# One gathered row in sixteen chunks moves from GpSimd's indirect DMA to 128 single fetches issued by SyncE

## The chip, the cores and the metric

The kernel runs on one core of a Trainium2 chip. The metric is the device time of one execution in microseconds (us). The kernel before takes 6118.95 us (median of 10 runs, 6115.97 to 6129.21); the profiled execution took 6118.65 us, of which the profile's span, from the first to the last instruction, is 6116.9 us.

Engines are named as in the profile: PE (TensorE, matmul), PEld (its weight load), DVE (VectorE), ACT (ScalarE), POOL (GpSimd), SP (SyncE, which here does nothing but issue DMAs and wait).

## What is computed

Two layers of a "metaformer" on x of 4 images x 128 channels x 128 x 128 positions, float32. Cut to what matters:

```python
# layer 0
x = x + deform_conv(ln_c(x), w_off, w_conv)      # 3x3 deformable convolution
t = tokens(x); t = t + moe_top2(ln_t(t), router_w, router_b, expert_w, expert_b)
# layer 1
x = x + conv(ln_c(x), alphas)                     # a 1x1 mixing with a reversal of rows and columns
t = tokens(x); t = t + moe_by_expert(ln_t(t), gate_w, gate_b, weight1, weight2)

def bilinear_gather(x, py, px):                   # in deform_conv, for each of 9 taps
    y0, x0 = floor(py), floor(px)                 # py, px: position + tap + learned offset
    return sum of 4 corners of x at (y0|y0+1, x0|x0+1), each times its bilinear weight
```

Each output position needs, for each of 9 taps, four neighbouring input positions (128 channels each) at an address that is known only at run time.

## The kernel before, in words

**The table.** For each image a table in DRAM holds, at each of 129 x 130 positions, the 256 floats (1 KB) of two normalised pixels above each other. Two neighbouring entries, 2 KB, are the four corners of one sample. `positions` (L651) computes the index of every sample into `im.index`, a [128, 128, 9] int32 tile (x on the partitions, then row y and tap k).

**The gathers.** Each image is worked in 32 groups of four rows (`row_groups`, L162), each group in 9 chunks, one for each tap: 4 x 32 x 9 = 1152 chunks. `Chunk.gather` (L771) issues four indirect DMAs on POOL, one for each row of the chunk; each brings 128 x 2 KB (256 KB) into a quarter of a tile `g`. There are 4608 of them. `g` has AHEAD = 6 buffers (L248), and the gathers are recorded six chunks ahead of their use.

**A chunk's way.** `weighted` (L784) multiplies three of its rows by the corner weights on DVE; `weighted_too` (L792) multiplies the fourth, `g[:, 3]`, on ACT (for k > 0; for k = 0 DVE takes all four). `summed` (L800) transposes and adds the four corners on PE (16 matmuls `trg`), `moved` (L814) copies the result to `sT` on ACT, `convolved` (L734) multiplies by the tap's weights into `sums` on PE. After 9 taps `mixed` (L823) does the rest of the layers for the four rows.

**The order.** All work is recorded in one loop over chunks (two half-steps, "turns", a chunk), and `InOrder` (L94) keeps each engine's instructions in just this order. Jobs (`turns.start`) are generators that yield for a number of turns. Tiles and semaphores are placed by a framework; a DMA issued from SP or ACT takes one of eight completion semaphores in rotation, and is not issued before the DMA eight places earlier, which used the same semaphore, has landed.

**SP's queue.** SP issues, in order, for every group the load of its four input rows (`xg`, 256 KB) and the store of its result (`x_d`, 256 KB); while the next image's table is built (`block`, L530), one load `xc` (512 KB) and one store `table<-ent` (1 MB) for each 8 rows; in the last image also expert weights (`w<-in_weight`, `pad<-in_weight`), and the last pass over finished images (`w<-x_d`, `out<-w`, 512 KB each). It waits, in that order, for whatever each of these needs.

**Padding tiles.** `padding` (L458) copies transposed rows into one of four tiles `pads` (L332), which `offsets` (L467) reads three times shifted for the offset convolution. Later the four are room for expert weights (`flat_pads`, L335, in `rooms` L1655 and `others` L1680).

Of the kernel before, what the change touches and what calls it, by code (L numbers as in the profile page):

```python
# [42 lines left out]
F32 = mybir.dt.float32  # L43
I32 = mybir.dt.int32
U32 = mybir.dt.uint32
AF = mybir.ActivationFunctionType
ALU = mybir.AluOpType
AX = mybir.AxisListType
# [3 lines left out]
P = 128  # L52
# [5 lines left out]
HID = 512  # L58
# [6 lines left out]
TAPS = 9  # L65
EPS_C = 1e-6
EPS_T = 1e-5
RB = 8
CB = 16
TW = P + 1  # L70
TC = P + 2
# [14 lines left out]
BANKS = 6  # L86
AFTER = 11
SPACE = 13
BLOCK = 84
FILL = "fill"  # L90
DONE = "done"
# [98 lines left out]
def metaformer_kernel(  # L190
# [50 lines left out]
    with ExitStack() as main:  # L241
# [100 lines left out]
        blank = wts.tile([P, P], F32, name="blank")  # L342
        nc.vector.memset(blank, 0.0)
        flip = wts.tile([P, P], F32, name="flip")
        nc.gpsimd.memset(flip, 0.0)
        for base in (0, -P):
# [108 lines left out]
                yield from with_bias(ew_sb[:, 4 * h : 4 * h + 4, :], biases[h])  # L455


        def padding(t, h, row, read, padded):  # L458

            yield FILL  # L460
            tr = transposes(row, 4)
            read.append(h)
            yield turns.hop
            eng.scalar.copy(pads[(2 * t + h) % 4][:, :, 1 : P + 1], tr)
            padded.append(h)

        def offsets(im, t, padded):  # L467

            while len(padded) < 2:
                yield 1  # L470
            yield 1


            yield FILL
            po = bank([P, 4, P], "po")
            for k in range(3):
                for h in range(2):
                    eng.tensor.matmul(
                        po[h * P // 2 : (h + 1) * P // 2],
                        lhsT=woff_sb[:, k, :],  # L480
                        rhs=pads[(2 * t + h) % 4][:, :, k : k + P],
                        start=(k == 0),
                        stop=(k == 2),
                    )
            yield turns.hop
# [13 lines left out]
            yield turns.hop  # L499
            if i0 == 0:  # L500
                im.z[q] = pa.tile([P, CB + 2, 6 * TAPS], F32, name=f"z{im.b}_{q}", tag="z")
                if q == 0:
                    eng.vector.memset(im.z[q][:, 0, :], 0.0)
                else:
                    eng.scalar.copy(im.z[q - 1][:, CB + 1, :], tr[:, 0, 0, 0 : 6 * TAPS])
            eng.scalar.copy(
                im.z[q][:, 1 + i0 : 1 + i0 + RB, :].rearrange("p (h i) o -> p h i o", h=2),
                tr[:, :, :, 0 : 6 * TAPS].rearrange("p i h o -> p h i o"),
            )
            if i0 == 0 and q > 0:  # L510
# [192 lines left out]
        class Group:  # L703
# [30 lines left out]
            def convolved(self, k):  # L734

                yield 1
                if k + 1 < FIRST:
                    return
                if k + 1 == FIRST:
                    eng.tensor.matmul(  # L740
                        sums.rearrange("p s c -> p (s c)"),
                        lhsT=blank,
                        rhs=iota,
                        start=True,
                        stop=False,
                    )
# [13 lines left out]
                if k + 1 == TAPS:  # L760
                    yield turns.hop
                    yield from mixed(self)

        class Chunk:


            def __init__(self, group, k):
                self.group, self.k = group, k
                self.shared = k > 0

            def gather(self):  # L771
# [12 lines left out]
            def weighted(self):  # L784
                n = 3 if self.shared else 4
# [4 lines left out]
                )  # L790

            def weighted_too(self):  # L792
                g, y = self.g[:, 3], self.group.rows[3]
                w = self.group.im.weight[y // CB]
                for v in range(4):
                    eng.scalar.activation(
                        g[:, v, :], g[:, v, :], AF.Copy, scale=w[:, y % CB, self.k, v : v + 1]
                    )

            def summed(self):  # L800

                self.tr = bank([P, 4, P], "trg")
                for s in range(4):
                    for v in range(4):
                        eng.tensor.matmul(
                            self.tr[:, s, :],
                            lhsT=self.g[:, s, v, :],
                            rhs=ident,
                            is_transpose=True,
                            start=(v == 0),  # L810
                            stop=(v == 3),
                        )

            def moved(self):  # L814
# [2 lines left out]
                eng.scalar.copy(group.sT[self.k], self.tr)  # L817
                turns.start(group.convolved(self.k))


        exps = []

# [766 lines left out]

        def in_turn():  # L1590

            for b in range(NB):
                for number, (rows_of, minus, runs) in enumerate(orders[b]):
                    im = images[b]
                    if im.sent <= P // RB or not im.weight.keys() >= {y // CB for y in rows_of}:
                        raise ValueError("a table is late")
                    group = Group(images[b], number, rows_of, minus, runs)
                    group.begin()
                    for k in range(TAPS):
                        chunk = Chunk(group, k)  # L1600
                        chunk.gather()
                        yield chunk

        source = in_turn()
        chunk = [next(source) for _ in range(AHEAD)]
        turns.hop = HOP
# [5 lines left out]
        def tick(more):  # L1612

            turns.fills(0)
            turns.slot += 1
            if more and total - QUICK <= n <= total:
                turns.steps()
                turns.fills(0)
                turns.slot += 1

        while n < total + 3 or turns.jobs:
# [134 lines left out]
```

## Time and profile before

| | us |
|---|---|
| median of 10 runs | 6118.95 |
| profiled execution | 6118.65 |
| its span | 6116.9 |
| PE busy | 5444.3 (89%) |
| DVE busy | 4846.0 (79%) |
| POOL busy | 4467.9 (73%) |
| ACT busy | 3821.4 (62%) |
| software DMA queue (POOL's gathers), share of 16 DMA engines | 64.4% |
| hardware DMA queue (SP's transfers, and ACT's few), share of 16 DMA engines | 14.2% |

A POOL instruction `DMA_INDIRECT g<-table,index` is the making of one gather's descriptors; the transfer itself runs on the 16 DMA engines afterwards. For SP, the profile lists only the issue of a DMA (named SPq); "to landing" is the time from the start of the issue until the last of the data is there.

### The profile page before, as it was taken

What the parts mean: (1) busy time and instruction counts of PE and PEld (TensorE: products, weight loads), DVE (VectorE), ACT (ScalarE), POOL (GpSimd) and SP (SyncE); (2) the same over time, 40 slices, a digit from 0 to 9 for tenths busy, and PEclk for the clock granted to TensorE, in tenths of its full rate; (3) what the DMA queues carried; (4) which work ended last, traced back from release to release, by engine and by line L of the source; (5) the groups of instructions that cost most, each with busy time, mean ns of one, the idle gap of its engine ahead of it and who ended that gap; (6) DMA issues with size and microseconds to landing.
All of it is one profiled execution on the core that took longest, in us unless ns stands there. A gap on an engine that the chain in (4) does not pass through costs nothing.

```text
span 6116.9 us, 118020 instructions
## 1 busy us (share of the span) xinstructions
PE 5444.3 (89%) x38823; PEld 4444.7 (73%) x38823; DVE 4846.0 (79%) x15420; ACT 3821.4 (62%) x9910; POOL 4467.9 (73%) x4795
## 2 busy tenths in 40 slices
PE   6899999998899999988889999999888998999984
PEld 4777777777777777777777777777777687777763
DVE  5688888887788888887778888888788787888872
ACT  4566666665666666666666666666655565666652
POOL 5777777777777777777777777777777777777750
PEclk8999999999999999999999999999999999999987
DMA  7778787877777777777777778777777897999777
GB/s 234 228 238 256 240 254 243 254 236 224 240 242 242 247 240 246 251 235 224 230 246 247 240 245 248 238 244 250 221 227 214 292 339 217 323 340 321 224 227 273
DMA packets 579234, 1526.15 MB, mean 249 GB/s; under 512 B 86456, under 2 KB 225408, under 8 KB 578624
## 3 DMA queue, kind: packets, MB, share of 16 engines
q0 software_dynamic: 369664, 1210.35, 64.4%
q1 hardware_dynamic: 206656, 299.87, 14.2%
q8 instruction: 310, 5.08, 0.3%
q10 hardware_dynamic: 2304, 8.39, 0.3%
q14 instruction: 300, 2.46, 0.1%
HBM read 1381.43 MB, written 136.85 MB: 248 GB/s over the span
## 4 chain that ended last, share of the span: by engine, by line
PE 30%; DMA 26%; DVE 16%; ACT 10%; issue 9%; POOL 9%; DVEq 0%; ACTq 0%; POOLq 0%; SPq 0%
DMA g<-table,index 23%; PE trg L104 10%; PE sums L104 9%; POOL g L104 8%; PE pe L104 6%; DVE g L104 5%; DVE x L104 5%; ACT g L104 4%; PE po L104 2%; PE tr L104 2%; DMA out<-w 2%; ACT sT L104 1%; ACT L104 1%; ACT xn L104 1%; PE small L104 1%
## 5 line engine op out<-in xcount | busy, mean ns | idle before, releaser
L104 POOL DMA_INDIRECT g<-table,index x4608 | 4368.7, 948 | 1409.5 <-issue 985.1
L104 DVE TENSOR_TENSOR g<-g,small 128x1536 f32<-128x1536 f32 (+1 forms) x1152 | 2083.1, 1809 | 901.4 <-DMA g<-table,index 773.3
L104 PE MATMUL trg<-ident,g 128*128 128x128 f32 x18432 | 2266.5, 277 | 155.2 <-DVE g L104 63.4
L104 PEld LDWEIGHTS trg<-ident,g 128*128 128x128 f32 x18432 | 2102.5, 144 | 275.1 <-DVE g L104 68.7
L104 ACT ACTIVATE g<-g,weight 128x128 f32<-128x128 f32 x4096 | 1306.2, 391 | 842.8 <-DMA g<-table,index 832.6
L104 DVE SCALAR_TENSOR_TENSOR x<-pe,gate,x 128x128 f32<-128x128 f32 x4072 | 1388.9, 343 | 83.3 <-PE pe L104 29.9
L104 PEld LDWEIGHTS sums<-wconv_sb,sT 128*128 128x128 f32 x9216 | 1139.6, 194 | 333.1 <-ACT sT L104 179.2
L104 PE MATMUL sums<-wconv_sb,sT 128*128 128x128 f32 x9216 | 1215.5, 280 | 131.8 <-ACT sT L104 130.3
L104 PE MATMUL pe<-ew_sb,nT 128*128 128x512 f32 x2048 | 1052.3, 612 | 177.4 <-ACT sT L104 151.2
L104 ACT COPY sT<-trg 128x512 f32<-128x512 f32 x1152 | 653.2, 568 | 98.6 <-PE trg L104 97.6
L104 PEld LDWEIGHTS pe<-ew_sb,nT 128*128 128x128 f32 x2048 | 330.8, 194 | 349.7 <-ACT sT L104 202.4
L104 ACT ACT_TABLE_LOAD x263 | 337.4, 1283 | 7.5 <-DVE nmax L104 2.2
L104 ACT ACTIVATE xn<-x,c_nb,c_rs 128x128 f32<-128x128 f32 x512 | 211.3, 485 | 167.3 <-DVE c_nb L104 167.2
L104 ACT ACTIVATE n<-x,b_nb,b_rs 128x128 f32<-128x128 f32 x512 | 210.3, 482 | 129.8 <-DVE b_nb L104 62.9
L104 ACT ACTIVATE c_rs<-c_mv,eps_c 128x4 f32<-128x4 f32 x128 | 37.9, 296 | 401.6 <-DVE c_mv L104 398.3
L104 ACT ACTIVATE tn<-x,d_nb,d_rs 128x128 f32<-128x128 f32 x512 | 210.9, 483 | 75.2 <-DVE d_nb L104 75.1
L104 PE MATMUL po<-pad,woff_sb 128*64 128x512 f32 x768 | 193.0, 621 | 21.8 <-DVE x L104 19.2
L104 PEld LDWEIGHTS sums<-ident,xg 128*128 128x128 f32 x1024 | 151.7, 212 | 77.7 <-issue 77.1
L104 ACT ACTIVATE ent<-raw,a_nb,a_rs 128x128 f32<-128x128 f32 x384 | 158.0, 484 | 16.1 <-DVE a_nb L104 14.3
L104 PEld LDWEIGHTS ps<-aT_sb,xfT 128*128 128x128 f32 x1024 | 130.1, 197 | 47.5 <-ACT xfT L104 37.1
L104 PE MATMUL ps<-aT_sb,xfT 128*128 128x128 f32 x1024 | 142.7, 284 | 22.0 <-ACT xfT L104 19.2
L104 PE MATMUL sums<-iota,blank 128*128 128x512 f32 x256 | 157.6, 702 | 0.0
(236 smaller groups left out, 5126.6 us busy)
## 6 DMA issues: line engine op xcount, KB each, us to landing
g<-table,index POOLq DMA_INDIRECT x4608, 3.8
table<-ent SPq DMA_DIRECT2D x48, 1024.0 KB, 6.4
xc<-in_x SPq DMA_DIRECT2D x64, 512.0 KB, 6.5
w<-x_d SPq DMA_DIRECT2D x64, 512.0 KB, 6.6
xg<-in_x SPq DMA_DIRECT2D x124, 256.0 KB, 7.3
x_d<-x SPq DMA_DIRECT2D x124, 256.0 KB, 4.2
out<-w SPq DMA_DIRECT2D x48, 512.0 KB, 8.0
w<-in_weight SPq DMA_DIRECT2D x42, 512.0 KB, 10.2
```

What stands on the lines that cost most here:

```text
L104: return self.tc.keep_in_program_order(issue(*args, **kwargs))
```

## The change

About one row in 64 is no longer gathered by POOL. For one chunk in sixteen, the fourth row is fetched by SP, in 128 DMAs of 2 KB, one for each x. This is done 71 times. A class `Lone` plans it while the program is recorded: it picks the user chunk n, a tap k > 0, so that the row is ready some eight chunks before; DVE multiplies the 128 indices by 1024 (bytes of a table entry); SP stores them in DRAM (`found`) and loads them again as a [4, 32] tile (`places`); then, for every 16 of them, one instruction loads 16 SP registers, and 16 DMAs follow, each from a register's byte offset in the table to one partition of a row tile. Five such DMAs are recorded each turn, so a row's 128 DMAs spread over 26 turns (13 chunks) of the 32 turns of a period. They stand in SP's queue among the other transfers.

Two of the four padding tiles (`pads[2:]`, "apart") become the two row tiles. In the main loop `padding` then has two tiles, and waits while they are in use (`busy`); as room for expert weights the two are replaced by two buffers of the pool `pw`. The tile `blank` goes, `zeros` takes its place.

```diff
+        apart = [
+            pad.rearrange("p y x -> p (y x)")[:, 0:HID].rearrange("p (v c) -> p v c", c=P)
+            for pad in pads[2:]
+        ]
+        busy = [False, False]
+        places = [wts.tile([4, P // 4], I32, name=f"places{i}") for i in range(2)]
+        scaled = [wts.tile([P, 1], I32, name=f"scaled{i}") for i in range(2)]
...
+        def pad_of(t, h):
+            return pads[(2 * t + h) % 4 if turns.hop == 1 else h]
+
         def padding(t, h, row, read, padded):
+            while turns.hop > 1 and busy[h]:
+                yield 1
+            busy[h] = True
             yield FILL
...
             def gather(self):
                 self.g = pg.tile([P, 4, 4, P], F32, name="g", tag="g")
                 im = self.group.im
                 for s, y in enumerate(self.group.rows):
+                    if s == 3 and self.lone is not None:
+                        continue
                     eng.gpsimd.indirect_dma_start(
...
+            def last(self):
+                return self.g[:, 3] if self.lone is None else self.lone
...
+        class Lone:
+            def __init__(self):
+                self.found = dram.tile([total // RUN + 2, P], I32, name="found")
+                self.tiles, self.users, self.end = {}, [], 0
+                self.ahead = self.filling = None
+            def look(self, t):
+                i, begin = len(self.users), max(t + 16, self.end)
+                n = (begin + 2 * RUN + 9) // 2 + 1
+                n += n % TAPS == 0
+                b, k = divmod(n, slots)
+                number, k = divmod(k, TAPS)
+                if n >= total or b not in images or i > 1 and begin <= 2 * self.users[-2]:
+                    return
+                im, y = images[b], orders[b][number][0][3]
+                if im.sent <= P // RB or im.known <= y // CB:
+                    return
+                self.users.append(n)
+                self.tiles[n] = apart[i % 2]
+                self.end = begin + 2 * RUN
+                self.ahead = self.job(i, n, im, im.index[:, y, k : k + 1], begin)
+            def job(self, i, n, im, index, begin):
+                row = self.found[i]
+                eng.vector.tensor_scalar(scaled[i % 2], index, 8.0 * P, None, ALU.mult)
+                yield
+                yield
+                eng.sync.dma_start(out=row.unsqueeze(1), in_=scaled[i % 2])
+                for _ in range(7):
+                    yield
+                eng.sync.dma_start(out=places[i % 2], in_=row.rearrange("(a c) -> a c", a=4))
+                while self.now < begin:
+                    yield
+                self.filling, self.ahead = self.ahead, None
+                flat = im.table.rearrange("e c -> (e c)").bitcast(U8)
+                for p in range(P):
+                    if p % 16 == 0:
+                        a, c = divmod(p, P // 4)
+                        loads, values = nc.values_load_multi_w_load_instructions(
+                            places[i % 2][a : a + 1, c : c + 16],
+                            engines=[mybir.EngineType.SP], ...
+                        )
+                    eng.sync.dma_start(
+                        out=apart[i % 2][p : p + 1]
+                        .rearrange("p (h v) c -> p h (v c)", h=2).bitcast(U8),
+                        in_=flat[bass.ds(values[p % 16], 16 * P)]
+                        .rearrange("(o h c) -> o h c", o=1, h=2),
+                    )
+                    if p % (P // (2 * RUN) + 1) == P // (2 * RUN):
+                        yield
+            def turn(self, t):
+                self.now = t
+                if self.filling is not None and next(self.filling, DONE) is DONE:
+                    self.filling = None
+                if self.ahead is None:
+                    self.look(t)
+                if self.ahead is not None:
+                    next(self.ahead)
...
             if 0 <= n < total:
                 chunk[n].summed()
                 turns.fill()
+                lone.turn(2 * n)
             tick(False)
...
             turns.steps()
+            if 0 <= n < total:
+                lone.turn(2 * n + 1)
...
-                rooms = [[part(), part()], [part(), part()], flat_pads]
+                rooms = [[part(), part()], [part(), part()], flat_pads[0:2]]
+                rooms[-1] += [spare(), spare()]
```

In the built programs POOL's DMAs fall by 71, SP's instructions for DMAs grow from 687 to 9917, of which 9088 are the single fetches; 568 register loads (16 registers each) come to SP, and 71 multiplications to DVE.

More of the change, by code (lines that the diff above doesn't have):

```diff
@@ L45 @@
 U32 = mybir.dt.uint32
+U8 = mybir.dt.uint8
 AF = mybir.ActivationFunctionType
@@ L88 @@
 SPACE = 13
+RUN = 16
 BLOCK = 84
@@ L339, in metaformer_kernel @@
         gb_sb = wts.tile([P, 1], F32, name="gb_sb")
-        blank = wts.tile([P, P], F32, name="blank")
-        nc.vector.memset(blank, 0.0)
         flip = wts.tile([P, P], F32, name="flip")
@@ L463, in padding @@
             yield turns.hop
-            eng.scalar.copy(pads[(2 * t + h) % 4][:, :, 1 : P + 1], tr)
+            eng.scalar.copy(pad_of(t, h)[:, :, 1 : P + 1], tr)
             padded.append(h)
@@ L480, in offsets @@
                         lhsT=woff_sb[:, k, :],
-                        rhs=pads[(2 * t + h) % 4][:, :, k : k + P],
+                        rhs=pad_of(t, h)[:, :, k : k + P],
                         start=(k == 0),
@@ L484, in offsets @@
                     )
+            busy[:] = [False, False]
             yield turns.hop
@@ L741, in convolved @@
                         sums.rearrange("p s c -> p (s c)"),
-                        lhsT=blank,
+                        lhsT=zeros[:, 0:P],
                         rhs=iota,
@@ L769, in __init__ @@
                 self.shared = k > 0
+                self.lone = None
             def gather(self):
@@ L792, in weighted_too @@
             def weighted_too(self):
-                g, y = self.g[:, 3], self.group.rows[3]
+                g, y = self.last(), self.group.rows[3]
                 w = self.group.im.weight[y // CB]
@@ L803, in summed @@
                 for s in range(4):
+                    g = self.g[:, s] if s < 3 else self.last()
                     for v in range(4):
@@ L806, in summed @@
                             self.tr[:, s, :],
-                            lhsT=self.g[:, s, v, :],
+                            lhsT=g[:, v, :],
                             rhs=ident,
@@ L818, in moved @@
                 turns.start(group.convolved(self.k))
+        class Lone:
[3 more added lines that the diff above has]
+                self.ahead = self.filling = None
+                self.values = []
+            def look(self, t):
[26 more added lines that the diff above has]
+                flat = im.table.rearrange("e c -> (e c)").bitcast(U8)
+                values = []
+                for p in range(P):
[3 more added lines that the diff above has]
+                            places[i % 2][a : a + 1, c : c + 16],
+                            engines=[mybir.EngineType.SP],
+                            min_val=0,
+                            max_val=8 * P * (TW * TC - 2),
+                            skip_runtime_bounds_check_because="positions are clamped to the table",
+                        )
+                        for load in loads:
+                            tc.keep_in_program_order(load)
+                    eng.sync.dma_start(
+                        out=apart[i % 2][p : p + 1]
+                        .rearrange("p (h v) c -> p h (v c)", h=2)
+                        .bitcast(U8),
+                        in_=flat[bass.ds(values[p % 16], 16 * P)]
[3 more added lines that the diff above has]
+                        yield
+                if self.now >= 2 * n - 2:
+                    raise ValueError("a row is late")
+            def turn(self, t):
[6 more added lines that the diff above has]
+                    next(self.ahead)
@@ L1590, in in_turn @@
         def in_turn():
+            n = 0
             for b in range(NB):
@@ L1600, in in_turn @@
                         chunk = Chunk(group, k)
+                        chunk.lone = lone.tiles.get(n)
+                        n += 1
                         chunk.gather()
                         yield chunk
+        lone = Lone()
         source = in_turn()
@@ L1653, in metaformer_kernel @@
                 part = lambda: late.tile([P, 2, HID], F32, name="w", tag="w", bufs=4)
-                rooms = [[part(), part()], [part(), part()], flat_pads]
+                spare = lambda: pw.tile(
+                    [P, 1, HID], F32, name="w", tag="weight", bufs=3 * P // CB // 2
+                )
+                rooms = [[part(), part()], [part(), part()], flat_pads[0:2]]
+                rooms[-1] += [spare(), spare()]
                 rooms.append([pw.tile([P, 2, HID], F32, name="w", tag="index")])
```

## The prediction

> **What bounds the kernel now.** I read the page's table of engines first, then its list of costly groups, then POOL's own timeline and the table by stages.
>
> ```profile
> PE 5444.3 (89%) x38823; PEld 4444.7 (73%) x38823; DVE 4846.0 (79%) x15420; ACT 3821.4 (62%) x9910; POOL 4467.9 (73%) x4795
> ...
> L104 POOL DMA_INDIRECT g<-table,index x4608 | 4368.7, 948 | 1409.5 <-issue 985.1
> ...
> L104 ACT ACTIVATE g<-g,weight 128x128 f32<-128x128 f32 x4096 | 1306.2, 391 | 842.8 <-DMA g<-table,index 832.6
> ```
> ```profile
> 2999.46 0.95 POOL L104 DMA_INDIRECT g<-table,index  x1 [0.30 <-issue]
> 3000.71 0.95 POOL L104 DMA_INDIRECT g<-table,index  x1 [0.30 <-PE pe L104]
> 3001.96 0.94 POOL L104 DMA_INDIRECT g<-table,index  x1 [0.30 <-issue]
> ```
> ```profile
> 1500.00:1750.00 250.00, 225.83 (x1596) 186.18 (x1597) 198.99 (x622) 160.81 (x419) 189.08 (x200) 0.97 0.78 240
> 5250.00:5500.00 250.00, 231.80 (x1737) 198.75 (x1736) 205.78 (x583) 156.88 (x402) 189.01 (x200) 0.99 0.95 334
> ```
>
> PE is busiest, yet POOL sets the pace. Its 73% is misleading: before each gather stand 0.30 us that no event explains, so a gather costs 1.25 us start to start. 4608 x 1.25 = 5760 us; the first starts at 119.7, the last at 5921.4 us, so POOL issues without a break. The stage table (columns: PE, PEld, DVE, ACT, POOL busy, clock, DMA share, GB/s) shows exactly 200 POOL instructions in 250 us early and late. ACT waited 832.6 us for gathered rows and DVE 773.3: about 0.7 us a chunk, so the consumers have room. One gather removed is worth 1.25 us.
>
> **What is removed.** 71 gathers x 1.25 = 88.75 us. From the profiled 6118.65 (0.3 us under the median of 6118.95) that gives 6029.9 if everything new is hidden. In a period of sixteen chunks POOL then needs 63 x 1.25 = 78.75 us instead of 80.0. The consumers must go 1.6% faster, 0.08 us a chunk against the 0.7 us they wait: covered.
>
> **What is added on SP.** In the same 78.75 us SP must issue 128 fetches. The trace has no fetch of one row at a register's address; I bound it by SP's own issues.
>
> ```profile
> 51.15 0.97 SPq L104 DMA_DIRECT2D eb_bc<-in_expert_b  x2
> 52.17 0.44 SPq L104 DMA_DIRECT2D wconv_sb<-in_w_conv  x1
> 52.65 0.43 SPq L104 DMA_DIRECT2D aT_sb<-in_alphas  x1
> ```
> ```profile
> 1547.80 1.12 SPq L104 DMA_DIRECT2D table<-zeros  x2
> 1548.96 1.67 SPq L104 DMA_DIRECT2D xc<-in_x  x2
> ```
> ```profile
> L104 SPq DMA_DIRECT2D table<-zeros x8: 462/594/702, 2.9 to 2990.9; - x8
> ...
> DMA to landing us min/median/max: 4.4/4.4/4.4
> ```
> ```profile
> L104 SPq DMA_DIRECT2D x_d<-x x132: 326/366/1192, 291.0 to 5980.5; - x132
> L104 SPq DMA_DIRECT2D w<-x_d x64: 319/320/1200, 5151.1 to 6099.1; - x64
> ```
>
> A lone issue takes 0.32 us at least (w<-x_d). Three in a row with 128 partitions each go from 51.15 to 52.65: 0.50 us a piece, of which some 0.04 is the gap. The smallest transfers SP has are the borders' second halves, 2 KB in two rows: the pair took 1.12 us, the 256 KB first half 0.46 (the minimum of that tile's eight), the gap 0.05, so 0.61 for 2 KB. A small transfer is thus not a cheap issue. Lower end 0.32 + 0.04 = 0.36 us, upper end 0.70 + 0.04 = 0.74 (the slowest of those eight). I take the 2 KB row as the nearest in size and in the number of rows: 0.61 + 0.04 = 0.65 us. Then for one period:
>
> - fetches: 128 x 0.65 = 83.2 us;
> - SP's other transfers: in the built program 31 stand among 256 gathers, two added index transfers a row included, 7.7 a period x 0.45 (between x_d's median of 0.37 and the 0.50) = 3.5 us;
> - eight loads of 16 registers, not in the trace: nothing to 0.65 each (as a small transfer), 0 to 5.2, I take the middle, 2.6 us;
> - waits for a completion semaphore. There are eight, so a DMA isn't issued before the eighth before it has landed, and the fetches now come behind every large transfer within eight. Eight issues last 8 x 0.65 = 5.2 us. Landing takes 7.3 us for xg, 6.4 for table<-ent, 6.5 for xc (page, DMA issues), so 2.1, 1.2 and 1.3 too long, 1.8, 1.1 and 1.1 times a period: 6.5 us, nothing where two stand within eight; half, 3.2 us.
>
> Sum 92.5 us against POOL's 78.75. No slack of some chunks helps against a rate: each of 71 rows comes 13.75 us later, and the chunk that needs it holds ACT, PE, then through six buffers POOL. 6029.9 + 71 x 13.75 = 7006, said as 7000 us. With the lower ends (128 x 0.36 = 46 + 3.5 + 9 of such waits = 59 us) SP has room and the time is 6030; with the upper ones (94.7 + 3.5 + 5.2 + 3.7 = 107) 6029.9 + 71 x 28.3 = 8040.
>
> What queues behind SP's waits: xg, x_d, xc and table<-ent stand in the same queue, so they are late by as much as the fetches; xg is asked for nine chunks ahead, and x_d only frees a tile. All slip together, so they add nothing beside the period.
>
> The DMA page of the Trainium skill (DMA: Bandwidth & Descriptors, Rules for kernel authors) speaks against the change: many small transfers should be one large one, since under 64 KB one pays mostly overhead. The trace agrees as far as it goes: 256 KB gathered costs POOL 1.25 us, while 2 KB costs SP 0.61. By the rule alone the change loses; the rows decide only how much. The same page (Latency and other measured facts) gives a register load (tensor_load) a floor of about 600 ns; no run here shows one; eight would be 4.8 us in place of 2.6, an estimate that would make the sum 7160.
>
> **Edits at nothing.** 71 multiplications of 128x1 on DVE, as nmax's 128x1 (152 ns): 11 us on an engine that waits 773 us for gathers; uncovered, 11 us. `zeros` for `blank`: the same matmul. Two padding tiles for four: `padding` holds a pair from a copy (0.58 us in the rows of the tile pad) to the last of six matmuls (0.59), some three to ten turns of 2.5 us, and the next table block comes after about 30 turns (13 between the first image's later blocks); without that cover it would be a few us for each of 64 blocks, with PE's 0.7 us slack ahead of it. The two `pw` buffers for weights: a few loads land elsewhere, as many and as large as before.
>
> **The rivals.**
>
> *SP keeps up (6030 us).* It decides where the spacing is below 0.52 us: 128 x 0.52 = 66.6 + 3.5 + 2.6 + 5.4 of semaphore waits = 78.1. For it: the three issues in a row at 0.50, and that one descriptor could be quicker than 128. Against it: the 2 KB rows at 0.61, and a register address that has to be resolved.
>
> *SP keeps up until the last image (6360 us).* Between 5250 and 5500 us SP already carries 27 w<-x_d, 27 out<-w, 5 xg and 5 x_d, landing in 6.7, 8.8, 10.9 and 7.1 us: 20 a period. At a spacing of 0.50 the waits are 8.5 x 2.7 + 8.5 x 4.8 + 1.6 x 6.9 + 1.6 x 3.1 = 80, half 40 us; 64 + 8 + 2.6 + 40 = 115, 36 us too long, for the some 9.3 periods after 5151 us: +335 on 6030. For it: the DMA share of 0.95 there. Against it: many of these transfers stand next to each other and share a wait. It needs the spacing under 0.52 too.
>
> *SP's lateness just eats the gain (6119 us):* a period of 80.0 us, a spacing near 0.54.
>
> **How the numbers follow.** Overloaded throughout, the forecast, 7000 us: 0.46, its own range 6300 to 8040. Overloaded in the last image only: 0.20. SP keeps up: 0.31. Even: 0.03. A measurement of this kernel tells about 0.2% (12 us) from no change: faster 0.31, same 0.03, slower 0.66. The range starts at 6025, just under the full gain, and ends at 7700; what is left out is the upper part of the overload and a gain above 89 us.
>
> **What would show it.** Right: SP's issues of pad<-table spaced 0.6 us or more without waiting, POOL's gathers with idle time before them for a DMA, and a row's 128 fetches lasting longer than 64 us. Wrong: 200 gathers per 250 us still. For the second rival: 200 up to 4250 us, fewer after. A spacing under 0.52 us, or periods whose fetches wait only for producers, makes the forecast wrong.

## The result, and the profile after

The changed kernel takes 6380.84 us (median of 8 runs, 6368.85 to 6386.58), the kernel before 6118.75 beside it (28 runs): a ratio of 1.0423, with 95% interval 1.0414 to 1.0432. It is 262 us slower. The profiled runs have spans of 6382.2 and 6116.9 us, a difference of 265.3.

First the engines and two costly groups, from the page after.

```profile
PE 5515.0 (86%) x38823; PEld 4504.0 (71%) x38823; DVE 4838.2 (76%) x15490; ACT 3811.5 (60%) x9910; POOL 4400.5 (69%) x4724
...
L106 POOL DMA_INDIRECT g<-table,index x4537 | 4301.9, 948 | 1740.5 <-issue 1057.5
...
L106 ACT ACTIVATE g<-g,weight 128x128 f32<-128x128 f32 x3812 | 1215.0, 392 | 707.2 <-DMA g<-table,index 666.3
```

POOL has 71 gathers fewer, each as long as before (948 ns), and is busy 67 us less. But it idles 1740.5 us before its gathers instead of 1409.5. More than the relief was given back as waiting. The table by stages tells when (columns: length; PE, PEld, DVE, ACT, POOL busy and how often; clock, DMA share, GB/s):

```profile
1500.00:1750.00 250.00, 222.08 (x1573) 185.66 (x1572) 191.97 (x594) 156.04 (x405) 183.50 (x195) 0.95 0.82 234
3000.00:3250.00 250.00, 223.18 (x1592) 185.17 (x1590) 195.29 (x616) 160.19 (x422) 185.37 (x197) 0.97 0.83 239
5000.00:5250.00 250.00, 204.25 (x1715) 164.00 (x1716) 145.54 (x441) 115.40 (x295) 132.86 (x141) 0.87 0.76 234
5500.00:5750.00 250.00, 194.89 (x1303) 164.61 (x1303) 161.04 (x459) 122.89 (x313) 143.00 (x153) 0.88 0.83 264
```

POOL makes 195 to 197 gathers in 250 us early, 141 and 153 late, where it made 200 throughout. PE's granted clock is lower there too (0.87 and 0.88; 0.95 and 0.97 before), yet PE is busy only 195 to 204 of the 250 us, less than in any earlier stage shown. Counted by chunks (ACT's copies sT<-trg; three images are 864 chunks), the 265 us have two homes:

```
span in us            to 1st chunk   first three images   last image   tail
before                   138.6             4331.0           1463.2     184.2
after                    148.4             4386.2           1663.5     184.1
difference                +9.8              +55.2           +200.3      -0.1
```

Since 53 of the 71 rows lie in the first three images, POOL's relief alone would have made that stretch 66 us shorter; it is 55 longer. So about 120 us were lost there, and about 220 in the last image.

What one fetch costs SP stands in the rows of the row tiles and of `places` (duration min/median/max in ns):

```profile
L106 SPq MOVE pad<-table x9088: 29/29/38, 151.3 to 6140.8; - x198
L106 SPq DMA_DIRECT2D pad<-table x9088: 217/228/2253, 151.4 to 6140.9; - x198
...
L886 SPq TENSOR_LOAD <-places x568: 1132/1240/4353, 150.1 to 6134.2; - x190
```

A fetch issues in 0.228 us with a MOVE of 0.029 us; in an undisturbed stretch fetches stand 0.32 us apart, 0.37 on the mean of the 96% of steps under 1.2 us. That is about my lower end of 0.36, so SP should have kept up. Its own list of waits (total us, times, longest) shows what it does with the time:

```profile
SPq L106 <- DMA found<-scaled: 421.4, 68, 8.6
SPq L106 <- DVE scaled L106: 352.8, 50, 18.0
SPq L106 <- DMA pad<-table: 200.5, 424, 2.8
```

The 352.8 us for `scaled` are spare time: SP stands at the next row's store before its indices are made. So SP isn't overloaded in most of the program. The 421.4 us are new, 6.2 us a time for a store of 512 bytes. SP's timeline at one such store shows who waits:

```profile
2054.82 0.37 SPq L106 DMA_DIRECT2D found<-scaled  x1
2055.28 1.52 SPq L106 DMA_DIRECT2D pad<-table  x5
2056.86 0.37 SPq L106 DMA_DIRECT2D xc<-in_x  x1
2057.32 24.94 SPq L106 DMA_DIRECT2D pad<-table  x30
2082.36 0.25 SPq L106 DMA_DIRECT2D places<-found  x1
```

The store lands only after 9.5 us (median of the 71). `places`, which reads it back, comes 27 us later, when the store has long landed. The one that waits is the eighth DMA after the store, a fetch that takes the same completion semaphore: of the 30 fetches, the first is issued at 2057.32 us and the second at 2064.81.

POOL's timeline just after this store (columns: start, length, idle before it and its releaser):

```profile
2064.06 0.95 POOL L106 DMA_INDIRECT g<-table,index  x1 [0.30 <-DMA g<-table,index]
2067.68 0.94 POOL L106 DMA_INDIRECT g<-table,index  x1 [2.67 <-DMA g<-table,index]
2070.02 0.94 POOL L106 DMA_INDIRECT g<-table,index  x1 [1.39 <-DMA g<-table,index]
2071.27 0.95 POOL L106 DMA_INDIRECT g<-table,index  x1 [0.31 <-ACT g L106]
```

Some ten us after the store POOL stands still twice, 2.37 and 1.09 us longer than its 0.30, each time for the landing of an earlier gather. The DMA engines' own view of the 40 us from 2050 (slices of 1 us: busy share in tenths, then GB/s) shows why:

```profile
DMA  7776767999728674198999999867687677878977
GB/s 238 225 197 188 213 221 242 105 139 61 29 33 41 45 57 61 37 184 326 406 418 391 385 385 375 293 238 236 188 223 244 211 234 207 244 197 268 350 244 227
```

Two us after the store the rate falls from 242 GB/s to between 29 and 139 and stays there for ten us; in the first three of them the engines are marked full while they move 61 to 139. Then comes a burst of some 400 that makes good what was held up.

### The profile page after: what moved, and what is told of

The parts are those of the page before. It is cut to its first block, busy times and chain, and to the rows that moved or that the text cites. A ratio compares the mean times of both kernels' runs of the same rounds, so it can differ in the third digit from the quotient of the medians.

```text
span 6382.2 us, 137034 instructions
## 1 busy us (share of the span) xinstructions
PE 5515.0 (86%) x38823; PEld 4504.0 (71%) x38823; DVE 4838.2 (76%) x15490; ACT 3811.5 (60%) x9910; POOL 4400.5 (69%) x4724
## 4 chain that ended last, share of the span: by engine, by line
PE 29%; DMA 28%; DVE 18%; issue 8%; ACT 8%; POOL 7%; SPq 2%; another core or an unknown queue 0%; DVEq 0%; ACTq 0%; POOLq 0%
DMA g<-table,index 19%; PE trg L106 10%; PE sums L106 8%; DVE g L106 7%; POOL g L106 6%; PE pe L106 5%; DVE x L106 5%; ACT g L106 2%; DMA out<-w 2%; DMA pad<-table 2%; PE po L106 2%; PE tr L106 2%; SPq L106 1%; DMA w<-in_weight 1%; DMA w<-x_d 1%
## 5 line engine op out<-in xcount | busy, mean ns | idle before, releaser
L106 POOL DMA_INDIRECT g<-table,index x4537 | 4301.9, 948 | 1740.5 <-issue 1057.5
L106 ACT ACTIVATE g<-g,weight 128x128 f32<-128x128 f32 x3812 | 1215.0, 392 | 707.2 <-DMA g<-table,index 666.3
L106 PEld LDWEIGHTS sums<-wconv_sb,sT 128*128 128x128 f32 x9216 | 1154.8, 196 | 316.1 <-issue 157.3
L106 ACT ACTIVATE tn<-x,d_nb,d_rs 128x128 f32<-128x128 f32 x512 | 210.9, 483 | 70.4 <-DVE d_nb L106 68.6
L106 PE MATMUL pf<-ident,w 128*128 128x128 f32 x512 | 84.7, 312 | 104.5 <-DMA w<-x_d 58.9
L106 ACT COPY w<-pf 128x512 f32<-128x512 f32 x64 | 37.2, 586 | 228.1 <-DMA out<-w 134.0
```

The source lines that it names most:

```text
L106: return self.tc.keep_in_program_order(issue(*args, **kwargs))
```

## The experiments

In six of the eight sets of runs, the kernel before itself took 7616 to 7747 us, at a granted clock of 0.88 to 0.89 in place of 0.96. On this second kind of chip POOL doesn't set the pace (shown below), so the times decide little about its relief. Their traces hold only about a third of the landing records that the others hold (wide_store 35706, wide_store_2 103679), so a wait may have lost the record that explains it; their landings and waits are compared only with one another. Ratios are always to the kernel before on the same chip, with 95% interval.

**1. The index store as rows of 256 bytes, and no rows in the last image: one, the other, both.** `wide_store` repeats each index 64 times, so that the store writes 128 pieces of 256 bytes instead of 128 pieces of 4:

```diff
-        scaled = [wts.tile([P, 1], I32, name=f"scaled{i}") for i in range(2)]
+        scaled = [wts.tile([P, P // 2], I32, name="scaled")] * 2
-                self.found = dram.tile([total // RUN + 2, P], I32, name="found")
+                self.found = dram.tile([total // RUN + 2, P, P // 2], I32, name="found")
-                eng.sync.dma_start(out=row.unsqueeze(1), in_=scaled[i % 2])
+                eng.sync.dma_start(out=row, in_=scaled[i % 2])
-                eng.sync.dma_start(out=places[i % 2], in_=row.rearrange("(a c) -> a c", a=4))
+                eng.sync.dma_start(out=places[i % 2], in_=row[:, 0].rearrange("(a c) -> a c", a=4))
```

`bulk_only` plans no row for the last image (53 rows remain); `bulk_wide` has both edits:

```diff
-                if n >= total or b not in images or i > 1 and ...
+                if n >= total or b >= LATE or b not in images or i > 1 and ...
```

`store_alone` keeps all 71 stores and loads of indices, but fetches nothing; POOL makes all 4608 gathers:

```diff
+                yield
+                return
                 flat = im.table.rearrange("e c -> (e c)").bitcast(U8)
...
-                        chunk.lone = lone.tiles.get(n)
+                        chunk.lone = None
```

> Fetched rows in the first three images only; the last image gathers all rows on POOL as before. Theory 1 (in the last image SP's queue is overloaded: large transfers and fetches hold each other up through the eight completion semaphores): the last image, 1663 us from its first chunk to its last in the changed kernel, goes back to the 1463 us of the kernel before, so about 6381 - 200 = 6180 us; the first three images keep their loss of 55 us. Rival (the padding tiles and the other room for expert weights cost the time in the last image): it stays near 6380.

> The 128 indices are stored to DRAM as 128 rows of 256 bytes (64 copies of each) in place of 128 pieces of 4 bytes, and read back from the first of each; the rest as in the changed kernel. Theory 2 (the store of 4-byte pieces holds the DMA engines: the gathers issued about it land after 8 to 13 us in place of 4, and POOL, which may have eight gathers under way, stands still 2 to 3.5 us a row): no such gap of POOL is left in the first three images, which take about 4386 - 120 = 4265 us, so 6381 - 120 to 140 = 6240 to 6260. Rival (9088 fetches load one DMA engine, and this delays the gathers): 6380, gaps as before.

> Both edits together: fetched rows in the first three images only, indices stored in 256-byte rows. If theories 1 and 2 both hold and add: 6119 less some 54 rows x 1.25 us, and up to 10 us of a later start: 6050 to 6065 us, under the kernel before. If the fetches themselves cost something in the first three images: 6100 to 6180.

> All 4608 gathers stay on POOL and no row is fetched; only the store of the 71 index rows in 4-byte pieces and their way back are done, with the two padding tiles of the change. This measures the store by itself. Theory 2: POOL stands still 2 to 3 us at each store, 71 times: 6119 + 140 to 210 = 6260 to 6330 us, since POOL has no time to make good. Rival (the store is hidden, the fetches are what delays the gathers; the padding tiles cost nothing): 6119 us.

Measured, with 7747 us before: bulk_only 7725.32 (0.9985, 0.9969 to 1.0), wide_store 7775.94 (1.0043, 1.0026 to 1.006), bulk_wide 7728.93 (0.9976, 0.9963 to 0.999), store_alone 7738.61 (0.999, 0.9973 to 1.0006). As times they decide little. The landings of the gathers, taken from the traces, decide much:

```
median us from a gather's issue to the last landing record of its semaphore,
gathers issued 0 to 2 us after an index store
after 11.3     bulk_only, store_alone 10.7 to 10.9     wide_store, bulk_wide 3.6
(after: 3.8 before the store, 4.5 again 16 us after it)
```

With the store alone and not one fetch the gathers are late as in the changed kernel; with pieces of 256 bytes they aren't. The store does it, and it is its form, not its size: the 256-byte form writes 64 times as much. The two forms differ in one more thing: 128 pieces of 4 bytes all lie within 512 bytes of DRAM, 128 pieces of 256 fill 32 KB. Whether the size of the pieces or their closeness does the harm wasn't told apart.

**2. The same, meant for a chip where POOL sets the pace.** `bulk_wide_2` and `wide_store_2` repeat two of them.

> Both edits together again (fetched rows in the first three images only, indices stored in 256-byte rows), on a chip where the kernel before takes 6119 us. Theories 1 and 2 (SP's overload in the last image; the store of 4-byte pieces) hold and add: 6050 to 6065 us. If the fetches themselves cost something in the first three images: 6100 to 6180.

> The indices stored in 256-byte rows, all 71 rows fetched, on a chip where the kernel before takes 6119 us. Theory 2 (the store of 4-byte pieces holds the gathers back): the first three images take about 4265 us in place of 4386, the whole 6240 to 6260. Rival (one DMA engine loaded by the fetches): 6380. On a chip where the kernel before takes some 7600 to 7750 us, with PE idle for nothing that the profile shows, both give 7630 to 7780: only the landing of the gathers about the store tells them apart there.

bulk_wide_2 met the second kind, with 7629.35 before: 7667.52, 1.0042 (1.0007 to 1.0077). Its stages show that POOL doesn't pace such a chip:

```profile
1500.00:1750.00 250.00, 202.39 (x1296) 162.40 (x1295) 166.50 (x540) 131.23 (x343) 147.33 (x156) 0.91 0.63 188
```

Only 156 gathers go by in 250 us. The same kernel ran later on a chip of the other kind (bulk_wide_6, below) with a span of 6057.2 us in place of 7667.2. PE is busy 6092.0 us here and 5400.7 there with the same 38823 matmuls, at a clock of 0.88 and 0.97: 691 us more, where the spans differ by 1610. Where the rest comes from the trace doesn't tell, since half the records of DVE's and ACT's semaphores are missing from it (6287 of 12794 and 2975 of 5996 are there).

wide_store_2 had a chip with 6127.43 before: 6187.56, 1.0097 (1.0068 to 1.0127), so the form of the store is worth some 190 us of the 262. Its stages:

```profile
1500.00:1750.00 250.00, 227.35 (x1632) 187.81 (x1631) 200.59 (x634) 165.27 (x432) 189.33 (x200) 0.98 0.80 247
...
5000.00:5250.00 250.00, 217.43 (x1625) 182.67 (x1623) 176.77 (x522) 130.18 (x337) 175.16 (x184) 0.92 0.76 240
5500.00:5750.00 250.00, 212.19 (x1475) 178.78 (x1473) 180.62 (x527) 136.28 (x353) 156.06 (x166) 0.92 0.82 270
```

Early there are again 200 gathers in 250 us, and the first three images last 4272.0 us, 114 less than in the changed kernel. That fits POOL's standing still: where two gathers start over 1.3 us apart (250 to 4200 us) the changed kernel loses 120 us beyond 1.25 each, this one 7, the kernel before 7. All its fetches are there, so fetching alone doesn't make the gathers late. Late there are 184 and 166: a second cause remains, and this last image is 1594.9 us, 132 more than before.

**3. Whether the stores out<-w are late behind the fetches, and more of the same.** `out_on_act` issues the stores out<-w from ACT (`eng.scalar.dma_start` in place of `eng.sync`).

> Fetched rows in the first three images only, indices stored in 256-byte rows, where the kernel before takes some 6125 us. With wide_store_2 at 6188 us, theory 1 (SP's overload in the last image) expects the last image back at its old pace and the first three images with nearly their whole gain of 54 x 1.25 us: 6055 to 6075. If the fetches themselves cost in the first three images: 6100 or more.

> Fetched rows in the first three images only, indices still stored in 4-byte pieces. Theory 1: the last image back at 1463 us, the first three images 55 us over the kernel before: 6180 us. Rival (padding tiles and the room for expert weights cost the last image's time): 6380.

> All gathers on POOL, only the 71 stores in 4-byte pieces and their way back added. Theory 2: POOL stands still about 2 us at each: 6125 + 100 to 200 us. Rival (hidden): 6125.

> The changed kernel, but the 48 out<-w stores of the last image are issued by ACT in place of SP. If in the last image the out<-w stores are late because they stand behind fetches in SP's queue (ACT and DVE then wait for a tile w that the store has not read): the last image's 1663 us fall by 50 to 120, 6260 to 6330 us. Rival (fetches and stores only share the DMA engines, or the eight semaphores alone hold them): 6370 to 6390.

> Fetched rows in the first three images only, indices stored in 256-byte rows, on a chip where the kernel before takes some 6120 us. Theory 1 (SP's queue is overloaded in the last image): its last image back at 1463 us from wide_store_2's 1595, the first three as there, 59 us under the kernel before: 6055 to 6070. Rival (the padding tiles and the other room for weights cost the last image its time): 6180 to 6190, as wide_store_2.

> As bulk_wide_4: fetched rows in the first three images only, indices stored in 256-byte rows. Where the kernel before takes some 6120 us: theory 1 (SP's queue overloaded in the last image) 6055 to 6070; rival (padding tiles and the room for weights) 6180 to 6190. Where it takes some 7630 to 7750, PE sets the pace, and both give within 1% of it.

All met the second kind of chip (7626 to 7629 before): bulk_wide_3 7657.94 (1.0036, 1.0018 to 1.0054), bulk_only_2 7675.46 (1.006, 1.0028 to 1.0093), store_alone_2 7624.54 (0.9996, 0.9972 to 1.0019), out_on_act 7726.81 (1.0121, 1.0074 to 1.0167), bulk_wide_4 7660.85 (1.0032, 1.0011 to 1.0052), bulk_wide_5 7650.31 (1.004, 1.002 to 1.006). As tests of what they were made for, these missed. What they say: the stores of indices cost nothing measurable where POOL has time to spare (store_alone, twice), and the kernels with fetches in the first three images lie between 0.9976 and 1.006 of the kernel before. The changed kernel itself was never run on such a chip, so the 1.0121 of out_on_act says nothing of its edit.

**4. PE's work cut, to make POOL the bound.** So that POOL might set the pace on any chip, `cut_pool` leaves out three of four transposes of each gathered row and six of the convolution's taps, and fetches no row; `cut_wide` is `wide_store` with the same work left out, `cut_wide_act` also has out<-w on ACT. `bulk_wide_6` is `bulk_wide`, whole.

```diff
+                    if 2 <= i < TAPS - 1:
+                        continue
...
-                    for v in range(4):
-                            lhsT=g[:, v, :],
+                        lhsT=g[:, 0, :],
```

> PE is relieved, so that POOL sets the pace on any chip: one transpose of a chunk's four corners in place of four, and the tap matmuls of three taps in place of nine. No row is fetched, but the padding tiles and the room for expert weights are the change's. If these cost nothing: POOL's 4608 x 1.25 us and the ends, 6090 to 6120 us, 200 gathers in 250 us in the last image too. Rival (they cost the last image's time): the last image 1590 us or more, 6240.

> The same relief of PE, with all 71 rows fetched and the indices stored in 256-byte rows. Theory 1 (SP's queue overloaded in the last image): first three images 59 us under cut_pool, the last image 100 to 140 us over it, in all 40 to 80 us over cut_pool. Rival (PE's lack of room, not SP, is why the last image suffers): about 80 us under cut_pool.

> As cut_wide, and the 48 out<-w stores of the last image issued by ACT in place of SP. If the stores' place behind the fetches in SP's queue is the larger part of the loss: 60 us or more under cut_wide. If it is the eight completion semaphores, which all queues share, or the traffic: within 30 us of cut_wide.

> Fetched rows in the first three images only, indices in 256-byte rows, PE's work whole. Where the kernel before takes some 6120 us: theory 1, 6055 to 6070; rival (padding tiles, room for weights), 6180. Where PE sets the pace (before at 7600 or more): within 1% of the kernel before.

Here the chip was one where POOL sets the pace anyway (6117.96 before). cut_pool 6114.54 (0.9993, 0.9982 to 1.0004): with PE busy 175 of 250 us the time is the same, so PE did not bound it; its last image, with the new padding, zeros and weight buffers in place, is 1463.1 us as before (1463.2). cut_wide 6145.23 (1.0046, 1.0032 to 1.0059): last image 1559.7, 97 us over cut_pool. The two differ by the fetched rows and their index transfers alone, so these cost it, and the padding tiles and weight buffers nothing. cut_wide_act 6151.3 (1.0047, 1.0027 to 1.0066): last image 1562.1, no gain: the case of the semaphores or the traffic. (SP's and ACT's DMAs take the same eight semaphores; POOL's gathers have eight of their own.) The lists of waits of the two, cut_wide first, show where the wait went (cut_pool, without fetches, has 20.5, 10.8 and 22.3 in the order of the first list):

```profile
ACT w L106 <- DMA out<-w: 132.3, 30, 8.0
...
DVE w L106 <- DMA out<-w: 72.8, 18, 7.4
...
PE pf L106 <- DMA w<-x_d: 59.9, 19, 16.4
```
```profile
PE pf L106 <- DMA w<-x_d: 107.6, 31, 16.5
...
ACT w L106 <- DMA out<-w: 21.5, 12, 5.0
...
DVE w L106 <- DMA out<-w: 15.1, 5, 5.2
```

Once out<-w no longer stands in SP's queue, ACT and DVE wait less for it, 37 us in place of 205; but w<-x_d, still in that queue, keeps PE waiting longer, 107.6 in place of 59.9, and the time stays.

bulk_wide_6 takes **6056.8 us (two runs), a ratio of 0.9892 (0.9863 to 0.9921): it is faster than the kernel before.** Its stages:

```profile
3000.00:3250.00 250.00, 230.66 (x1657) 190.34 (x1657) 211.94 (x708) 171.64 (x452) 189.06 (x201) 0.99 0.81 249
...
5500.00:5750.00 250.00, 230.28 (x1617) 192.15 (x1616) 208.16 (x617) 155.47 (x406) 186.04 (x197) 0.96 0.80 258
```

The first three images last 4266.6 us, 64.4 less than before; 53 x 1.25 = 66.3. The last lasts 1467.7, with no fetch in it.

**5. The number of DMAs or their bytes.** `few` is `wide_store` with each 16 fetches in one DMA of the same bytes, from fixed rows of the table, so without register loads; `cut_few` leaves out PE's work as above, too.

```diff
+                    eng.sync.dma_start(
+                        out=apart[i % 2][p : p + 16].rearrange("p v c -> p (v c)"),
+                        in_=im.table[2 * p : 2 * p + 32].rearrange("(o h) c -> o (h c)", h=2),
+                    )
```

> As cut_wide, but each row's 2 KB pieces come in 8 DMAs of 16 partitions at fixed places of the table (so the fetched values aren't the sample's, and no registers are loaded): the same bytes, an eighth to a sixteenth of the issues and of the steps of the completion semaphores. Theory 1 (the number of DMAs in SP's queue, and their waits for eight semaphores): the last image 1440 to 1470 us, as cut_pool's 1463 less up to 20, against cut_wide's 1560; in all 6030 to 6060. Rival (the bytes of the fetches beside the weights and the last pass): the last image stays near 1560, 6150.

> The same with PE's work whole. Where the kernel before takes some 6120 us: theory 1, last image 1440 to 1480, in all 6030 to 6065, against wide_store_2's 6188; rival (bytes) 6180. Where PE sets the pace: within 1% of the kernel before.

Both met the second kind of chip, with 7615.97 before. cut_few takes 7140.29 (0.937, 0.9316 to 0.9424): PE's work counts here, 403 us between few and cut_few, where leaving it out saved 3 on the chip above; but leaving it out didn't make POOL the bound, so as a test of the last image's time it is inconclusive. few takes 7543.21 (0.9899, 0.9828 to 0.997), a gain, though none was expected of POOL's relief here; its last image is 1822.3 us where wide_store's was 1913.1 and that of store_alone, without fetches, 1863 to 1885 on other chips of this kind. The waits of wide_store, then of few:

```profile
ACT w L106 <- DMA out<-w: 81.9, 18, 9.2
...
DVE w L106 <- DMA out<-w: 51.2, 12, 10.6
...
PE pf L106 <- DMA w<-x_d: 36.5, 13, 16.2
```
```profile
PE pf L106 <- DMA w<-x_d: 26.6, 12, 16.5
...
ACT w L106 <- DMA out<-w: 15.5, 7, 4.9
...
DVE w L106 <- DMA out<-w: 14.0, 5, 5.6
```

They are back near the level of store_alone (22.4, 12.0, 10.0 in this order), which fetches nothing. The hardware queue moved the same bytes in as many packets in both kernels (320.89 MB, 244428), so these waits come with the number of DMAs in SP's queue (407 in the last image; 2491 in wide_store, 271 in store_alone). few drops the register loads as well, 138 in the last image x 1.24 = 171 us of SP's time, and reads the same rows of the table each time, so issues, loads and addresses aren't told apart by it. What the waits are worth in time where POOL sets the pace, no run of few shows.

## Why the prediction was wrong

Slower was right, but for another reason than the forecast's. 881 us was forecast, from an SP that can't issue the fetches in time; 262 came, from an index store that holds up others and from the last image's queue. That the direction agrees is luck: with the measured spacing my own sum gives 6030 us, a faster kernel.

**POOL's pace and the worth of a gather: right.** bulk_wide_6 got 64.4 of 66.3 us, so POOL did bound the kernel and the consumers had the room that I read from 0.7 us of waiting a chunk.

**The step that failed: "fetches: 128 x 0.65 = 83.2 us".** Measured, 128 x 0.37 = 47 us, short waits included. I took the two-row 2 KB store as the nearest row, for its size and its number of rows. In the changed kernel that store still takes 0.66 to 0.76 us, and a fetch of one row 0.228: an equal number of bytes didn't make the issues equal. My lower end of 0.36 was about the measured mean, and I passed it over. With it my own sum was 59 us a period, and I said that SP then has room. In the first three images it has: most of the 352.8 us spent waiting for `scaled` are that room. Of the signs I named, the spacing of 0.6 us didn't come. Rows of 128 fetches that last longer than 64 us did (77 us, the median of the first three images), but wide_store_2 has 75 there while POOL makes its 200 gathers, so that sign didn't tell what I took it to tell.

**"eight loads of 16 registers ... the middle, 2.6 us": too small.** They took 8 x 1.24 = 10 us, and my upper bound of 5.2 was too low as well. The Trainium skill (DMA: Bandwidth & Descriptors, Latency and other measured facts) gives about 0.6 us as the floor of a register load; this trace has 1.13 as the least for one of 16 registers, so the floor isn't the price.

**Semaphore waits, "half, 3.2 us": near in the first three images.** Between 1000 and 2300 us, some sixteen periods, SP's longest waits for xc, xg, x_d and table<-ent come to 26.5 + 18.5 + 11.8 + 11.3 = 68 us, 4.2 a period; waiting for `found` adds 6.2, of which I had nothing: I looked for landings too long among the large transfers, and the one of 512 bytes took 9.5 us. So a period is 47 + 3.5 + 10 + 4.2 + 6.2 = 71 us, within 78.75: the forecast's own mechanism, SP overloaded throughout, doesn't occur.

**The step that was missing: the index store's effect on others.** I costed the two index transfers as two of 7.7 issues at 0.45 us and went no further. The issue is 0.37 us, but the store holds up POOL's gathers; its 4-byte form cost 2.2 us a row in the first three images, (4386.2 - 4272.0) / 53. That term, which I had nowhere, turns -59 us into +55 in the first three images, and gives 68.6 more in the last. In the last image SP also waits 70.9 us for `found`; whether that or the late gathers make the 68.6 there wasn't told apart.

**The rival of the last image: the right place, with a wrong price.** It foresaw 200 gathers per 250 us until the last image and fewer after, and a loss of 335 us there against the gain of a kernel that keeps up. With the 256-byte store just this pattern is seen: 200, then 184 and 166, and a loss of 154 against full relief (131.7 + 18 x 1.25). Its term for waits, "half 40 us" a period, can be compared with SP's waits between 4700 and 6000 us in the changed kernel:

```profile
SPq L106 <- DMA w<-in_weight: 93.4, 59, 3.4
...
SPq L106 <- DMA w<-x_d: 61.7, 35, 4.5
SPq L106 <- DMA out<-w: 60.3, 28, 11.6
```

The weights, 93.4 us, were not in my list of transfers at all; out<-w and w<-x_d were. These three make 215 us in 1300, 13 us in 80, where I had put 40. How a queue with fetches between large transfers stands still shows in SP's timeline of that image:

```profile
5550.51 0.37 SPq L106 DMA_DIRECT2D out<-w  x1
5554.19 9.71 SPq L106 DMA_DIRECT2D pad<-table  x10
5564.15 0.36 SPq L106 DMA_DIRECT2D w<-x_d  x1
5564.61 2.68 SPq L106 DMA_DIRECT2D pad<-table  x5
5567.50 0.37 SPq L106 DMA_DIRECT2D out<-w  x1
```

After one out<-w it takes 3.3 us until the first fetch and 9.71 for ten of them, where ten take 3.2 in a quiet stretch. The w<-x_d behind them is issued 13.6 us after out<-w, and PE waits for such loads (58.9 us in all, 24.6 before). The trace names the semaphore of each wait. The first fetch waits for the one that an index store, issued eight DMAs earlier at 5545.04 us, raises until 5554.17; the second, issued at 5559.56, for that of a w<-x_d from 5545.49, raised until 5559.54. So these two waits are for the shared completion semaphores; how much of the last image's loss they make, apart from the issues and register loads, no run shows.

That this rival's 6360 us lies near 6381 is partly chance: the spans split into the store (6382.2 - 6192.4 = 190), the last image's queue (6192.4 - 6057.2 = 135) and the gain of bulk_wide_6 (-60). The rival had the second at more than twice its size and the first not at all.

**The edits at nothing: right.** cut_pool has the new padding, rooms and `zeros` and its last image is 1463.1 us against 1463.2, bulk_wide_6 has them with PE's work whole and takes 1467.7; store_alone, with the multiplications and the stores, stays within 0.1% where POOL has time to spare.

**Left open.** Why the kernel before takes 7616 to 7747 us in six sets of eight: it doesn't go by the chip's number, for chip 0 is listed once with 7628 and once with 6118, so it may not belong to the chip. How large the gain of `few` would be where POOL sets the pace, since it only met the second kind of chip. And whether the harm of the index store lies in the 4 bytes of its pieces or in their standing within 512.

## What to carry to other kernels

Price a transfer by what it does to the others as well as by its issue: look at how many bytes each of its pieces writes and how close they lie, at how long it takes to land if later DMAs share its semaphore, and at whose transfers are in the DMA engines at that time. Work moved to an idle queue is idle only by the stage: count, in the busiest stage, every large transfer that small ones would stand between, and leave that stage out if its transfers have consumers waiting. And when the nearest rows differ by a factor of two and none has the form of the new transfer, carry both through the sum: here they decided between an SP with room and one that can't keep up, and the row with the same bytes was the wrong one.

## What the runs showed of the hardware

A store of 128 pieces of 4 bytes, side by side in 512 bytes of DRAM, landed after 9.5 us (median), and gathers issued from another queue just after it took 11 us to land in place of 3.8. The same store as pieces of 256 bytes landed after 3.8 us and left the gathers near 4. In the 40 us around wide_store_2's store at 2078.08 us the rate shows no such hole (slices as above, from 2074):

```profile
GB/s 307 395 266 266 234 217 248 229 229 215 205 190 213 203 250 205 195 236 217 219 180 250 184 209 238 221 184 234 199 248 181 283 338 298 229 203 174 246 290 349
```

The share of POOL's queue in the DMA engines' time between 500 and 4200 us shows it as well, the changed kernel first, then wide_store_2:

```profile
q0 software_dynamic: 229496, 752.21, 71.5%
```
```profile
q0 software_dynamic: 235937, 773.30, 68.7%
```

Fewer packets took more of the engines' time. The Trainium skill (DMA: Bandwidth & Descriptors, Specifications) puts the line at 512 bytes, under which a DMA engine reads before it writes. The store of 4-byte pieces agrees in that it is dear, but pieces of 256 bytes, under that line too, didn't make the gathers late (medians of 3.6 to 4.0 us).

A DMA of one row at a register's address issues in 0.228 us, a third of a two-row one of the same 2 KB; a load of 16 registers took 1.24 us.
